# Two attention layers on one core: first key columns loaded first, and another order of copies, tables and products in the last passes

## Chip, core and metric

The kernel runs on one core of a Trainium2 chip. The metric is the time of one execution in microseconds (us) on the device. Before the change three runs gave 904.05, 904.2 and 906.41 us; the median is 904.2 us. All data are float32. Engines are called as in the profile: PE (TensorE's matrix products, PEld its weight loads), DVE (VectorE), ACT (ScalarE), POOL (GpSimd), SP (SyncE, which here only issues transfers). ACT and POOL issue transfers too.

## What is computed

Two cross-attention layers, one after the other, for 8 batches of 256 tokens with 320 channels, 20 heads of 16 channels, and a context of 256 tokens of 512 channels. Cut to what matters:

```python
# layer 0: first 77 context tokens are text, the other 179 image tokens
q = split(x @ Wq.T); k, v = split(text @ Wk.T), split(text @ Wv.T)
k_ip, v_ip = split(ip @ Wk_ip.T), split(ip @ Wv_ip.T)
a = softmax(q @ k.T / 4) @ v + softmax(q @ k_ip.T / 4) @ v_ip
x = x + merge(a) @ Wo.T + bo
# layer 1: first 252 context tokens are text, the last 4 image tokens
probs_t = softmax(q @ k_t.T / 4)
text_out = probs_t @ v_t
qsem = l2norm(probs_t @ text_ehs)                 # 512 channels per head and token
fused = q @ k_ip.T / 4 + 0.5 * (qsem @ l2norm(ip_ehs).T)
ip_out = (softmax(fused) * spatial_mask) @ v_ip
x = x + merge(text_out + ip_out) @ W_out + b_out
```

## The kernel before the change

**Work.** A unit is one batch, one layer and a quad of four heads. There are 40 units per layer (8 batches, 5 quads). The main loop (L1155) runs n from 0 to 45. For n below 40, `both_layers` (L1078) does unit n of layer 0 and, six steps behind (SHIFT), a unit of layer 1. For n = 40 to 45, `layer_1` (L1123) does layer 1 alone: n = 40 the last quad of batch 6, n = 41 to 45 the five quads of batch 7. `l1_end` (L863) finishes the last quad and the output of batch 7. Other work (projections, transposes, outputs) is put between the steps by `fillers` (L976), a table of functions by step and place: in n = 40 transposes, projections and keys, in n = 41 queries and keys, in n = 44 transposes and outputs; n = 42, 43 and 45 have no or hardly any PE work there.

**Order.** The order on PE, DVE, ACT and POOL is the program's own order. An engine runs its instructions one after the other and waits at each for what it needs. SP's order is chosen by the framework. Transfers are issued by SP, ACT and POOL, each in its own queue; eight semaphores for the transfers of SP and ACT are used in turn, so that a transfer can wait for an earlier one to land before it is issued.

**Start.** SP loads xT and encT of batch 0, then x and texts. ACT's queue (L160 to L166) loads wq, wk, wkip, the tails of wk and wkip (64 channels of layer 1's keys, L120), wv and wvip. The tile of wk holds 4 blocks of 128 rows with 320 + 64 columns. PE does q (`project_q`, L270; 12 PE instructions, since each float32 product is two), then 128 channels of keys (`project_k`, L288: a part with wk, a part with wkip), ACT copies them (L445), POOL makes a masked query (L332, tile qz, two buffers), and the scores of a quad follow (`scores`, L335), then the values v (`project_rows`, L302). Later loads are issued by POOL (`load_late`, L957).

**A unit of layer 1.** Its steps, with their lines:

- scores (L342): 16 PE instructions into four PSUM tiles sc, one per head j, with both halves of the tokens;
- `l1_max` (L693): per head one DVE reduction for the negative maximum (L696);
- `l1_exp` (L706): per head and half one exponential on ACT with its sum (L711; here "exp j0" means both halves of head 0);
- `l1_image_scores` (L688): per head a copy of the image scores out of sc (tile aip, L691);
- `l1_transposed` (L719, L380): four transposes per head, which write over sc, and a copy out (et, L387);
- `l1_values` (L722): per head and half a product y (L735 and L738) in one of two PSUM buffers, a DVE step e that multiplies and sums it (L742), and a copy of 20 numbers out of it (num, L746). A buffer is free for the next but one y when e and num of its y are done.

In `layer_1` a pass runs the scores, maxima, exponentials and transposes of its own unit u1, and the values of the unit before, v1. The order is:

```python
for pair in range(2):
    l1_max(u1, pair, False)
    l1_values(v1, pair, (0,), nc.scalar.copy)
    l1_exp(u1, pair)
    l1_values(v1, pair, (1,))
    fillers(n, 2 + pair)
```

then the four aip copies on ACT, place 4, the values of head 2, all four transposes with place 5 between them, the values of head 3, place 6.

**The end.** `l1_end` splits the 20 heads into the first 16 and the last 4. For each part: `l1_den` (L760) and `l1_norm` (L766: a DVE step L771, a square root on ACT L773, and a dummy exponential L776 that brings back ACT's table for Exp), `l1_text` (POOL, L814), `l1_fused` and `l1_fused_exp` (L785 to L794), `l1_probs` (L796), `l1_probs_T` (transposes L828, copy L835). The sums of text and image are made on PE: products of the text part with the identity (L884), then products with the image part (L893); `keep` copies them out (L902), `project` (L905) multiplies with Wo, L950 adds the residual, and SP and ACT store. ACT holds one table of functions at a time; a change between square root and exponential is a load (ACT_TABLE_LOAD).

Of the kernel before, what the change touches and what calls it, by code (L numbers as in the profile page):

```python
# [8 lines left out]
F32 = mybir.dt.float32  # L9
# [4 lines left out]
P = 128  # L14
# [3 lines left out]
NE = E // P  # L18
# [32 lines left out]
def kernel(  # L51
# [40 lines left out]
    def mm_tile(name):  # L92
        return ps_mm.tile([P, 512], F32, tag="mm", name=name)
# [15 lines left out]
    def new_e(name, pool=const, tag=None, again=0):  # L109
        return pool.tile([P, NE, C + again], F32, tag=tag or name, name=name)  # L110
# [5 lines left out]
    def load_e(t, w, eng):  # L116
        n = min(C, t.shape[2])
        eng.dma_start(out=t[:, :, 0:n], in_=w[:, 0:n].rearrange("(k p) c -> p k c", p=P))

    def load_tail(t, w, eng):  # L120

        eng.dma_start(
            out=t[:, :, C:], in_=w[:, C - HP :].rearrange("(k p) c -> p k c", p=P)
        )

    def load_xT(b, eng):
# [22 lines left out]
    wo, wo1 = new_c("wo"), new_c("wo1")  # L149


    wk, wkip = new_e("wk", again=HP), new_e("wkip", again=HP)
    wk1 = const.tile([P, NE, C - HP], F32, tag="wk1", name="wk1")

    wv, wvip, wv1 = new_e("wv"), new_e("wvip"), new_e("wv1", again=NIP)
# [2 lines left out]
    bo_b = const.tile([P, C], F32, tag="bo_b", name="bo_b")  # L158
    bo1_b = const.tile([P, C], F32, tag="bo1_b", name="bo1_b")
    load_c(wq, WqT, nc.scalar)  # L160
    load_e(wk, WkT, nc.scalar)
    load_e(wkip, WkipT, nc.scalar)
    load_tail(wk, Wk1, nc.scalar)
    load_tail(wkip, Wk1, nc.scalar)
    load_e(wv, WvT, nc.scalar)
    load_e(wvip, WvipT, nc.scalar)  # L166

    ident = const.tile([P, P], F32, tag="ident", name="ident")
    make_identity(nc, ident)
# [38 lines left out]

    def columns(w, k, m):

        return w[:, k, m * P : (m + 1) * P]

    twice(wq)
# [476 lines left out]
        ip = 0 if u["t0"][x] else TXT1  # L690
        copy(bat[u["b"]]["aip"][:, :, h, :], sc[:, :, ip : ip + NIP])  # L691

    def l1_max(u, x, image=True):  # L693
        t0 = u["t0"][x]
        for j in range(2):
            nc.vector.tensor_reduce(  # L696
                u["nmx"][x][:, j, :],
                u["sc"][2 * x + j][:, :, t0 : t0 + TXT1],
                AX.X,
                ALU.max,  # L700
                negate=True,
            )
            if image:
                l1_image_scores(u, x, j, nc.vector.tensor_copy)

    def l1_exp(u, x):  # L706
        t0 = u["t0"][x]
        for j in range(2):
            h = QUADS[u["g"]][1][2 * x + j]
            for half in range(NH):  # L710
                nc.scalar.activation(  # L711
                    u["e"][x][:, j, half, t0 : t0 + TXT1],
                    u["sc"][2 * x + j][:, half, t0 : t0 + TXT1],
                    AF.Exp,
                    bias=u["nmx"][x][:, j, half : half + 1],
                    accum_out=bat[u["b"]]["den1"][:, half, h : h + 1],
                )

    def l1_transposed(u, j, copy=None):  # L719
        transposed_probs(u, j, TC1, u["t0"][j // 2], copy)  # L720
# [39 lines left out]
    def l1_den(b, hs=ALL):  # L760
        r = bat[b]
        den = r["den1"][:, :, hs]
        nc.vector.reciprocal(by_head(r, "rden1", b)[:, :, hs], den)
        nc.vector.tensor_tensor(by_head(r, "nrm", b)[:, :, hs], den, den, ALU.mult)

    def l1_norm(b, hs=ALL):  # L766
        r = bat[b]
        n2 = r["n2"][:, :, hs]

        nrm = by_head(r, "nrm", b)[:, :, hs]  # L770
        nc.vector.scalar_tensor_tensor(nrm, nrm, EPS2, n2, ALU.mult, ALU.max)  # L771

        nc.scalar.activation(nrm, nrm, AF.Sqrt, scale=1.0 / SEM_SCALE**2)  # L773

        one = small.tile([P, 1], F32, tag="one", name=f"one_{b}", bufs=1)
        nc.scalar.activation(one, msk[:, 0:1], AF.Exp)  # L776

    def l1_fused(b, hs=ALL, eng=nc.gpsimd):
        r = bat[b]
# [38 lines left out]
                ALU.mult,  # L818
            )

    def l1_probs_T(b, hs=ALL, ps=None):
        r = bat[b]

        rows = hs.stop * NIP
        if ps is None:
            ps = mm_tile(f"pT_{b}")
        for half in range(NH):
            nc.tensor.transpose(  # L828
                ps[:rows, half * P : (half + 1) * P],
                r["fus"][:, half, : hs.stop, :].rearrange("p h k -> p (h k)"),  # L830
                ident,
            )
        if "pT" not in r:
            r["pT"] = small.tile([H * NIP, NH * P], F32, tag="pT", name=f"pT_sb_{b}", bufs=1)
        nc.vector.tensor_copy(r["pT"][:rows], ps[:rows, : NH * P])  # L835

    def l1_attn(b):
        r = bat[b]
# [24 lines left out]
    def l1_end(b, u):  # L863

        r = bat[b]
        first, last = slice(0, 16), slice(16, H)

        def tile(j, name):
            return ps_sc.tile([P, NH * S], F32, tag=f"sc{j}", name=f"end_{name}")

        def values(j, half):
            l1_values(u, j, (half,), nc.scalar.copy)
# [12 lines left out]

        def image(ps, ms, hs):
            rows = hs.stop * NIP  # L890
            vip = r["vip"].rearrange("p h d -> p (h d)")[:rows]
            for i, m in enumerate(ms):
                nc.tensor.matmul(  # L893
                    ps[:, i * S : (i + 1) * S], chunk(vip, m), r["pT"][:rows],
                    start=False, stop=m == ms[-1],
                )

        def keep(ps, ms):
            n = len(ms)
# [13 lines left out]
        o = [tile(2 + half, f"o_{half}") for half in range(NH)]  # L913
        l1_den(b)
        l1_norm(b, first)
        values(0, 0)
        l1_text(b, first)
        values(0, 1)
        l1_fused(b, first)
        values(1, 0)  # L920
        values(1, 1)
        l1_fused_exp(b, first)
        sums = tile(0, "aT")
        text(sums, (0, 1))
        values(2, 0)
        values(2, 1)
        l1_probs(b, first)
        values(3, 0)
        values(3, 1)
        l1_norm(b, last)  # L930
        l1_text(b, last)
        l1_probs_T(b, first, tile(1, "pT"))
        l1_fused(b, last, nc.vector)
        l1_fused_exp(b, last, nc.vector)
        image(sums, (0, 1), first)
        keep(sums, (0, 1))
        sums = mm_tile("end_aT2")
        text(sums, (2,))
        l1_probs(b, last, nc.vector)
        project(0, 0)  # L940
        project(0, 1)
        project(1, 0)
        l1_probs_T(b, last, tile(1, "pT2"))
        project(1, 1)
        image(sums, (2,), last)
        keep(sums, (2,))
        for half, eng in enumerate((nc.sync, nc.scalar)):
            project(half, 2)
# [118 lines left out]
    def part(f, u, *args):  # L1067
        if u is not None:
            f(u, *args)
# [53 lines left out]
    def layer_1(n, u, v1):  # L1123


        fillers(n, 0)
        fillers(n, 1)
        part(l0_attn, u)
        u1 = begin1(n)

        if (n + 1 - SHIFT) % NQ:
            qz[1] = queries(1, n + 1)
        for pair in range(2):
            l1_max(u1, pair, False)
            l1_values(v1, pair, (0,), nc.scalar.copy)
            l1_exp(u1, pair)
            l1_values(v1, pair, (1,))
            fillers(n, 2 + pair)
        for head in range(4):
            l1_image_scores(u1, head // 2, head % 2, nc.scalar.copy)  # L1140
        fillers(n, 4)
        part(l1_values, v1, 2)
        for head in range(4):
            if head == 2:
                fillers(n, 5)
            part(l1_transposed, u1, head, nc.scalar.copy)
        part(l1_values, v1, 3)
        fillers(n, 6)
        return None, u1

    l0_q(0, (0, 1))
# [77 lines left out]
```

## Time and profile before

| What | Value |
|---|---|
| median of three runs | 904.2 us |
| the profiled execution: its time | 902.27 us |
| its span in the profile | 900.6 us |
| PE busy | 867.4 us (96%) |
| DVE, ACT, POOL busy | 606.3 (67%), 550.1 (61%), 221.8 us (25%) |
| from 0 to 16.3 us: PE busy | 8.17 us |
| from 797.0 to 877.4 us: PE busy | 76.17 of 80.40 us |
| from 877.4 to 900.6 us: PE busy | 15.81 of 23.20 us |
| exponential of layer 1 (L711), 128 x 252 | 484 ns |
| maximum of layer 1 (L696), 128 x 504 | 673 ns |
| e (L742) and num on DVE (L746) | 418 and 174 ns |
| a table load on ACT | 1.28 us |

A line of the merged timeline gives start in us, length in us, engine, line, operation, written tile <- read tiles, shapes and count, and in brackets the idle time of the engine before it with what ended it. A line of the stretches gives length, busy time of PE, PEld, DVE, ACT and POOL with counts, the granted clock of PE, the mean share of the DMA engines and GB/s. A line of a DMA queue gives packets, MB and the share of 16 engines that the packets took. The chain of waits is followed back from the last instruction; its shares tell which engine's work set the end.

### The profile page before, as it was taken

What the parts mean: (1) busy time and instruction counts of PE and PEld (TensorE: products, weight loads), DVE (VectorE), ACT (ScalarE), POOL (GpSimd) and SP (SyncE); (2) the same over time, 40 slices, a digit from 0 to 9 for tenths busy, and PEclk for the clock granted to TensorE, in tenths of its full rate; (3) what the DMA queues carried; (4) which work ended last, traced back from release to release, by engine and by line L of the source; (5) the groups of instructions that cost most, each with busy time, mean ns of one, the idle gap of its engine ahead of it and who ended that gap; (6) DMA issues with size and microseconds to landing.
All of it is one profiled execution on the core that took longest, in us unless ns stands there. A gap on an engine that the chain in (4) does not pass through costs nothing.

```text
span 900.6 us, 18697 instructions
## 1 busy us (share of the span) xinstructions
PE 867.4 (96%) x6170; PEld 696.6 (77%) x6170; DVE 606.3 (67%) x2043; ACT 550.1 (61%) x2406; POOL 221.8 (25%) x397
## 2 busy tenths in 40 slices
PE   6999899999999999999999999999999999899996
PEld 4767678788777888788887788878877887678774
DVE  1454477767776777776777677776687767874664
ACT  3775666646654686556766468555775557745663
POOL 5522311213211232132221223212221223212201
PEclk9999999999999999999999999999999999999998
DMA  9500100001000100001001010001000100000000
GB/s 298 143 6 1 56 2 1 1 16 42 15 2 21 33 24 2 20 17 42 15 1 21 16 43 1 1 20 34 24 1 11 25 1 2 1 20 1 1 20 16
DMA packets 21072, 22.96 MB, mean 25 GB/s; under 512 B 5856, under 2 KB 20128, under 8 KB 20976
## 3 DMA queue, kind: packets, MB, share of 16 engines
q1 hardware_dynamic: 15072, 13.27, 5.8%
q10 hardware_dynamic: 4608, 4.38, 1.6%
q0 software_dynamic: 1296, 4.12, 1.5%
q8 instruction: 50, 0.82, 0.4%
q14 instruction: 46, 0.38, 0.1%
HBM read 18.31 MB, written 2.62 MB: 23 GB/s over the span
## 4 chain that ended last, share of the span: by engine, by line
PE 80%; ACT 6%; DVE 2%; issue 1%; POOL 0%; ACTq 0%; DVEq 0%
PE y L735 15%; PE sc L380 15%; PE sc L342 8%; PE v L305 8%; PE y L738 8%; PE k L293 6%; PE q L275 6%; PE p_o L318 5%; PE oT L513 4%; ACT e L495 2%; ACT e L711 2%; PE g L604 2%; PE p_aT_ps L311 1%; PE ipo L842 1%; PE o L533 1%
## 5 line engine op out<-in xcount | busy, mean ns | idle before, releaser
L495 ACT ACTIVATE e<-sc,nmx 128x77 f32<-128x77 f32 (+1 forms) x640 | 227.1, 411 | 57.5 <-DVE nmx L483 57.5
L711 ACT ACTIVATE e<-sc,nmx 128x252 f32<-128x252 f32 x320 | 147.0, 484 | 103.4 <-DVE aip L691 103.4
L735 PE MATMUL y<-gv,et 126*128 126x272 f32 x640 | 202.9, 398 | 5.0 <-ACT num L746 4.4
L742 DVE CUSTOM_DVE_ANT_0 e<-y,e 128x252 f32<-128x252 f32 x320 | 133.4, 418 | 108.2 <-PE y L738 96.4
L380 PE MATMUL sc<-ident,e 128*126 128x128 f32 (+1 forms) x1280 | 182.8, 275 | 11.8 <-ACT e L495 6.5
L483 DVE TENSOR_REDUCE nmx<-sc 128x2 f32<-128x154 f32 x320 | 109.6, 414 | 91.5 <-PE sc L342 91.5
L380 PEld LDWEIGHTS sc<-ident,e 128*126 128x126 f32 (+1 forms) x1280 | 148.1, 140 | 25.1 <-ACT e L495 12.5
L387 DVE COPY et<-sc 128x512 f32<-128x512 f32 (+1 forms) x222 | 149.9, 688 | 26.0 <-PE sc L380 16.8
L495 ACT ACTIVATION_READ_ACCUMULATOR e<-sc,nmx 128x1 f32 x640 | 159.7, 250 | 0.0
L738 PEld LDWEIGHTS y<-gv,et 126*128 126x128 f32 x640 | 121.1, 189 | 26.0
L738 PE MATMUL y<-gv,et 126*128 126x146 f32 x640 | 131.9, 288 | 0.0
L735 PEld LDWEIGHTS y<-gv,et 126*128 126x128 f32 x640 | 105.3, 191 | 22.7 <-ACT num L746 6.8
L548 POOL TENSOR_TENSOR attn<-o_sb 128x64 f32<-128x64 f32 x80 | 24.5, 327 | 396.9 <-DVE o_sb L538 357.0
L696 DVE TENSOR_REDUCE nmx<-sc 128x2 f32<-128x504 f32 x160 | 105.6, 673 | 24.2 <-PE sc L342 24.2
L387 ACT COPY et<-sc 128x512 f32<-128x512 f32 (+1 forms) x98 | 55.9, 587 | 75.4 <-PE sc L380 75.4
L342 PE MATMUL sc<-k,sc_qz 32*128 32x256 f32 x1152 | 83.4, 400 | 1.3 <-POOL sc_qz L332 0.8
L332 POOL TENSOR_SCALAR sc_qz<-q,quad_m 128x256 f32<-128x256 f32 x80 | 73.2, 926 | 10.2 <-ACT q L282 9.9
L342 PEld LDWEIGHTS sc<-k,sc_qz 32*128 32x128 f32 x1152 | 52.9, 184 | 24.7 <-issue 14.4
L711 ACT ACTIVATION_READ_ACCUMULATOR e<-sc,nmx 128x1 f32 x320 | 70.0, 219 | 0.0
L305 PE MATMUL v<-wv,encT 128*126 128x324 f32 (+1 forms) x192 | 58.1, 446 | 0.3 <-DMA wv<-in_WvT_dram 0.3
L318 PE MATMUL p_o<-wo,p_aT 128*128 128x320 f32 x180 | 52.8, 437 | 0.3 <-DVE p_aT L312 0.3
L746 DVE COPY num<-y 128x20 f32<-128x20 f32 x300 | 52.2, 174 | 0.0
(159 smaller groups left out, 1053.8 us busy)
## 6 DMA issues: line engine op xcount, KB each, us to landing
encT<-in_encT_dram SPq DMA_DIRECT2D x7, 512.0 KB
x<-in_x_dram SPq DMA_DIRECT2D x8, 320.0 KB
out_dram<-osb SPq DMA_DIRECT2D x15, 160.0 KB
xT<-in_xT_dram SPq DMA_DIRECT2D x7, 256.0 KB
texts<-in_encT_dram SPq DMA_DIRECT2D x6, 154.0 KB
xT<-in_xT_dram SPq DMA_DIRECT2D x7, 128.0 KB
vip_rows<-vipA SPq DMA_DIRECT2D x32, 25.0 KB
wk<-in_WkT_dram ACTq DMA_DIRECT2D x1, 640.0 KB
```

The costliest lines, as they stand in the source:

```text
L305: nc.tensor.matmul(ps, lhsT(k), w[:, k, :], start=(k == 0), stop=(k == NE - 1))
L318: nc.tensor.matmul(ps[:, :C], aT[:, m, :], w[:, m, :], start=(m == 0), stop=(m == NC - 1))
L342: nc.tensor.matmul(sc[j][:, half, :], qz[rows, half * P : (half + 1) * P], kT(j)[rows, :], start=True, stop=True,)
L380: nc.tensor.transpose(v[:, c, half, :], u["e"][x][:, i, half, t0 + c * tn : t0 + (c + 1) * tn], ident,)
L387: copy(u["et"][x][:tn, i].rearrange("p c n s -> p (c n s)"), ps)
L483: nc.vector.tensor_reduce(u["nmx"][x][:, j, :, a], u["sc"][2 * x + j][:, :, t0:t1], AX.X, ALU.max, negate=True,)
L495: nc.scalar.activation(u["e"][x][:, j, half, t0:t1], u["sc"][2 * x + j][:, half, t0:t1], AF.Exp, bias=u["nmx"][x][:, j, half, a : a + 1], ...
L696: nc.vector.tensor_reduce(u["nmx"][x][:, j, :], u["sc"][2 * x + j][:, :, t0 : t0 + TXT1], AX.X, ALU.max, negate=True,)
L711: nc.scalar.activation(u["e"][x][:, j, half, t0 : t0 + TXT1], u["sc"][2 * x + j][:, half, t0 : t0 + TXT1], AF.Exp, bias=u["nmx"][x][:, j, ...
L735: nc.tensor.matmul(y, et[:, 1 - odd, half, :], gv[0][:, g, full], start=True, stop=False)
L738: nc.tensor.matmul(y[:, into], et[:, odd, half, :], gv[1][:, g, part], start=False, stop=True)
L742: nc.vector.tensor_tensor_reduce(e, y[:, g0 : g0 + TXT1], e, op0=ALU.mult, op1=ALU.add, scale=1.0, scalar=0.0, accum_out=r["n2"][:, half, ...
```

## The change

At the start, wk and wkip become lists of two tiles: the first 128 columns, and the other 192 with the 64 tail columns. ACT issues wq and the two first tiles only; wv, wvip and the second tiles are issued by SP, behind encT and ahead of x and texts. Four products of zeros are put on PE ahead of q, and a dummy exponential on ACT ahead of its first copy. In the passes of layer 1 alone, maximum, exponentials and values go head by head with num of half 0 on DVE and of half 1 on ACT, and the values of head 2 come between the transposes of heads 0, 1 and of heads 2, 3; `l1_den` of the last batch is moved into the last pass. In `l1_end` num of heads 0 and 1 is copied by DVE, the square root's table is loaded by a dummy right after the first exponential, the identity products move behind the first part's transposes, and the last copy of pT is shared by DVE and ACT.

```diff
+    def load_part(t, at, w, c0, c1, eng):
         eng.dma_start(
-            out=t[:, :, C:], in_=w[:, C - HP :].rearrange("(k p) c -> p k c", p=P)
+            out=t[:, :, at : at + c1 - c0], in_=w[:, c0:c1].rearrange("(k p) c -> p k c", p=P)
         )
...
-    wk, wkip = new_e("wk", again=HP), new_e("wkip", again=HP)
+    wk, wkip = [
+        [const.tile([P, NE, n], F32, tag=f"{name}{n}", name=f"{name}{n}") for n in (P, C + HP - P)]
+        for name in ("wk", "wkip")
+    ]
...
     load_c(wq, WqT, nc.scalar)
-    load_e(wk, WkT, nc.scalar)
-    load_e(wkip, WkipT, nc.scalar)
-    load_tail(wk, Wk1, nc.scalar)
-    load_tail(wkip, Wk1, nc.scalar)
-    load_e(wv, WvT, nc.scalar)
-    load_e(wvip, WvipT, nc.scalar)
+    load_part(wk[0], 0, WkT, 0, P, nc.scalar)
+    load_part(wkip[0], 0, WkipT, 0, P, nc.scalar)
+    load_e(wv, WvT, nc.sync)
+    load_e(wvip, WvipT, nc.sync)
+    for w, given in ((wk, WkT), (wkip, WkipT)):
+        load_part(w[1], 0, given, P, C, nc.sync)
+        load_part(w[1], C - P, Wk1, C - HP, C, nc.sync)
+
+    zeros = work.tile([P, S], F32, tag="qz", name="zeros", bufs=2)
+    nc.vector.memset(zeros, 0.0)
+    ps = mm_tile("zeros")
+    for i in range(4):
+        nc.tensor.matmul(ps[:, :S], zeros[:, :P], zeros, start=True, stop=True)
+
+    one = small.tile([P, 1], F32, tag="one", name="one", bufs=1)
+    nc.vector.memset(one, 0.0)
+    nc.scalar.activation(one, one, AF.Exp)
...
     def columns(w, k, m):
+        if isinstance(w, list):
+            w, m = (w[0], 0) if m == 0 else (w[1], m - 1)
         return w[:, k, m * P : (m + 1) * P]
...
+    def table(func):
+        one = small.tile([P, 1], F32, tag="one", name="one", bufs=1)
+        nc.scalar.activation(one, msk[:, 0:1], func)
...
-        nc.vector.tensor_copy(r["pT"][:rows], ps[:rows, : NH * P])
+        if shared:
+            for copy, cols in ((nc.vector.tensor_copy, slice(0, P)), (nc.scalar.copy, slice(P, 2 * P))):
+                copy(r["pT"][:rows, cols], ps[:rows, cols])
+        else:
+            nc.vector.tensor_copy(r["pT"][:rows], ps[:rows, : NH * P])
...
-        l1_den(b)
         l1_norm(b, first)
-        values(0, 0)
         l1_text(b, first)
-        values(0, 1)
+        values(0, nc.vector.tensor_copy)
         l1_fused(b, first)
-        values(1, 0)
-        values(1, 1)
+        values(1, nc.vector.tensor_copy)
         l1_fused_exp(b, first)
-        sums = tile(0, "aT")
-        text(sums, (0, 1))
-        values(2, 0)
-        values(2, 1)
+        table(AF.Sqrt)
+        values(2, nc.scalar.copy)
         l1_probs(b, first)
-        values(3, 0)
-        values(3, 1)
+        values(3, nc.scalar.copy)
         l1_norm(b, last)
         l1_text(b, last)
         l1_probs_T(b, first, tile(1, "pT"))
         l1_fused(b, last, nc.vector)
         l1_fused_exp(b, last, nc.vector)
+        sums = tile(0, "aT")
+        text(sums, (0, 1))
         image(sums, (0, 1), first)
...
-        l1_probs_T(b, last, tile(1, "pT2"))
+        l1_probs_T(b, last, tile(1, "pT2"), True)
...
         for pair in range(2):
-            l1_max(u1, pair, False)
-            l1_values(v1, pair, (0,), nc.scalar.copy)
-            l1_exp(u1, pair)
-            l1_values(v1, pair, (1,))
+            for j, copy in ((0, nc.vector.tensor_copy), (1, nc.scalar.copy)):
+                l1_max(u1, pair, False, (j,))
+                l1_exp(u1, pair, (j,))
+                l1_values(v1, pair, (j,), copy)
             fillers(n, 2 + pair)
         for head in range(4):
             l1_image_scores(u1, head // 2, head % 2, nc.scalar.copy)
         fillers(n, 4)
-        part(l1_values, v1, 2)
-        for head in range(4):
-            if head == 2:
-                fillers(n, 5)
-            part(l1_transposed, u1, head, nc.scalar.copy)
-        part(l1_values, v1, 3)
-        fillers(n, 6)
+        for pair in range(2):
+            for head in (2 * pair, 2 * pair + 1):
+                l1_transposed(u1, head, nc.scalar.copy)
+            if n == N0 + SHIFT - 1 and pair:
+                l1_den(B - 1)
+            part(l1_values, v1, 2 + pair)
+            fillers(n, 5 + pair)
```

More of the change, by code (lines that the diff above doesn't have):

```diff
@@ L118, in load_e @@
         eng.dma_start(out=t[:, :, 0:n], in_=w[:, 0:n].rearrange("(k p) c -> p k c", p=P))
-    def load_tail(t, w, eng):
+    def load_part(t, at, w, c0, c1, eng):
         eng.dma_start(
-            out=t[:, :, C:], in_=w[:, C - HP :].rearrange("(k p) c -> p k c", p=P)
+            out=t[:, :, at : at + c1 - c0], in_=w[:, c0:c1].rearrange("(k p) c -> p k c", p=P)
         )
@@ L691, in l1_image_scores, with l1_max @@
         copy(bat[u["b"]]["aip"][:, :, h, :], sc[:, :, ip : ip + NIP])
-    def l1_max(u, x, image=True):
+    def l1_max(u, x, image=True, heads=range(2)):
         t0 = u["t0"][x]
-        for j in range(2):
+        for j in heads:
             nc.vector.tensor_reduce(
@@ L704, in l1_max, with l1_exp @@
                 l1_image_scores(u, x, j, nc.vector.tensor_copy)
-    def l1_exp(u, x):
+    def l1_exp(u, x, heads=range(2)):
         t0 = u["t0"][x]
-        for j in range(2):
+        for j in heads:
             h = QUADS[u["g"]][1][2 * x + j]
@@ L773, in l1_norm @@
         nc.scalar.activation(nrm, nrm, AF.Sqrt, scale=1.0 / SEM_SCALE**2)
-        one = small.tile([P, 1], F32, tag="one", name=f"one_{b}", bufs=1)
-        nc.scalar.activation(one, msk[:, 0:1], AF.Exp)
+        table(AF.Exp)
     def l1_fused(b, hs=ALL, eng=nc.gpsimd):
@@ L819, in l1_text, with l1_probs_T @@
             )
-    def l1_probs_T(b, hs=ALL, ps=None):
+    def l1_probs_T(b, hs=ALL, ps=None, shared=False):
         r = bat[b]
@@ L872, in tile, with values @@
             return ps_sc.tile([P, NH * S], F32, tag=f"sc{j}", name=f"end_{name}")
-        def values(j, half):
-            l1_values(u, j, (half,), nc.scalar.copy)
+        def values(j, copy):
+            for half in range(NH):
+                l1_values(u, j, (half,), copy)
         def chunk(t, m):
```

## The prediction

> **What bounds the kernel now.** I read the page's chain first: it says which engine set the end.
>
> ```profile
> PE 80%; ACT 6%; DVE 2%; issue 1%; POOL 0%; ACTq 0%; DVEq 0%
> ```
>
> TensorE carries the end, so an edit counts only where PE waits. The busy time by stretch shows where that is: PE is busy 767.24 of 780.70 us from 16.3 to 797 us, which the diff leaves alone, but 8.17 of 16.30 at the start, 76.17 of 80.40 in the passes of layer 1 alone (n = 40 to 45), 15.81 of 23.20 at the end. Those three are what is edited.
>
> The start, in PE's timeline (start, length, idle before and its releaser):
>
> ```profile
> 5.15 4.46 PE L275 MATMUL q<-xT,wq 128*128 128x256 f32 x12 [5.15 <-DMA wq<-in_WqT_dram]
> 10.42 1.09 PE L293 MATMUL k<-encT,wk 128*128 128x77 f32 x8 [0.81 <-DMA wk<-in_WkT_dram]
> 12.86 1.48 PE L293 MATMUL k<-encT,wkip 128*128 128x179 f32 x8 [1.35 <-DMA wkip<-in_WkipT_dram]
> 14.89 1.15 PE L342 MATMUL sc<-k,sc_qz 32*128 32x256 f32 x16 [0.55 <-ACT k L445]
> 16.30 2.39 PE L305 MATMUL v<-wv,encT 128*128 128x320 f32 x8 [0.27 <-DMA wv<-in_WvT_dram]
> ```
>
> The landing of wkip sets the first scores. The last pass (n = 45), from the merged timeline:
>
> ```profile
> 868.05 1.27 DVE L696 TENSOR_REDUCE nmx<-sc 128x2 f32<-128x504 f32 x2 [0.43 <-PE sc L342]
> ...
> 869.70 0.18 ACT L746 COPY num<-y 128x20 f32<-128x20 f32 x1 [3.42 <-DVE n L742]
> 869.77 0.48 ACT L711 ACTIVATE e<-sc,nmx 128x252 f32<-128x252 f32 x1
> ...
> 869.92 0.72 PE L735 MATMUL y<-gv,et 126*128 126x272 f32 x2 [0.28 <-ACT num L746]
> ...
> 873.73 0.39 ACT L691 COPY aip<-sc 128x8 f32<-128x8 f32 x4
> ...
> 873.97 1.97 PE L380 MATMUL sc<-ident,e 128*126 128x128 f32 x16 [0.20 <-ACT aip L691]
> ```
>
> The transposes (L380) wait for the first image copy (aip), which stands behind all eight exponentials on ACT. While PE waits it does the products y of heads 0, 1 and 2. The end:
>
> ```profile
> 880.65 0.20 ACT L776 ACTIVATE one<-msk 128x1 f32<-128x1 f32 x1
> 880.76 0.23 ACT L746 COPY num<-y 128x20 f32<-128x20 f32 x2
> ...
> 880.97 0.72 PE L735 MATMUL y<-gv,et 126*128 126x272 f32 x2 [1.86 <-ACT num L746]
> ```
>
> PE stands still because the copies that free its two y buffers sit behind a table load. What follows, by stretches (length, busy us of each engine, granted clock, DMA):
>
> ```profile
> 882.00:883.00 1.00, 1.00 (x6) 0.95 (x5) 0.45 (x3) 0.18 (x1) 0.00 (x0) 0.62 0.00 0
> 883.00:884.00 1.00, 1.00 (x6) 1.00 (x6) 0.59 (x3) 0.18 (x1) 0.33 (x1) 0.50 0.00 0
> ```
>
> After 1.86 us without work PE ran for 3.4 us at half clock.
>
> **Part 1, the loads.** ScalarE's queue loses wk, wkip, wv, wvip and two tails, and keeps 128 columns of wk and of wkip; wv, wvip and the rest go to SP ahead of x and texts. How two queues share the DMA engines, from 9.5 to 11.0 us (q10 is ScalarE's, q1 SP's; packets, MB, share):
>
> ```profile
> q10 hardware_dynamic: 315, 0.40, 83.4%
> q1 hardware_dynamic: 314, 0.10, 28.0%
> ```
>
> They take turns packet by packet: 315 packets of 1280 B against 314 of 308 B. A packet costs its engine 0.834 x 24 / 315 = 63.5 ns and 0.280 x 24 / 314 = 21.4 ns. The 1024 B packets of 6.00 to 7.25 us cost 48.6 ns (189 at 45.9% of 20 us); 512 B, between, are estimated at 29. wk and wkip are 1024 packets before and after, 1280 B before and 512 B after. Before, they began at 6.0: 202 went beside 189 of encT until 7.25, 286 beside 214 of x until 9.0, 536 one to one with the 308 B texts: 536 x 84.9 / 16 = 2.84, so 11.84; the product began 1.0 later. After, at the same ratios: 0.94, then (286 x 29 + 214 x 63.5) / 16 = 1.37, then 536 one to one with wv's 1280 B: 536 x 92.5 / 16 = 3.10. Sum 11.4, product at 12.4: 0.45 earlier. What the short rows save, SP's long rows take back. wv no longer lands last (0.27 before L305). I take **-0.7**. Bounds: if the queues shared by bytes, 2 x 0.91 MB would be through at 7.9 us by the GB/s row, and two products of 0.9 and 1.4 would give scores at 11.7, **-3.2**; if nothing lands earlier and the longer idle brings half clock, k and scores gain 1.2, **+1.2**.
>
> Covered: four zero products (eight instructions at 0.43, twice the warm 0.216) end before 5.15 and let q take 2.8 (the row of 2.79 at 143.22) for 4.46, but PE then waits for wk; the early table load (1.28 at 10.71) ended before k did. The remaining columns of wk and wkip stand in SP's queue beside POOL's loads (wk1 at 14.48 first); the DMA ran full until 22.4 and they are needed at 27.7, so nothing, unless over 5 us late. x and texts come later still, and x is used by POOL's adds after 34.65. SP's queue gains waits for reused semaphores: wvip's for xT (landed by 5.15), with all the rest behind it; the others' for wq and encT, which land before their turn. The zeros lie in a masked query's buffer, free long before POOL's second one (13.6).
>
> The Trainium skill ("DMA: Bandwidth & Descriptors", "Issuing engines are not separate DMA queues") says that issuing on several engines saves only issue time. That speaks against this part, and by it the sum would be 0.0 here; the packet counts say that a queue's row size matters, and give -0.7.
>
> **Part 2, the passes.** Now each head's maximum, exponentials and product follow each other, half 0's num copy is on DVE and half 1's on ACT; and heads 0 and 1 are transposed ahead of head 2's y. Times from the start of the scores (866.89). Before: exp 2.88, third y 3.03, fourth y 3.84, aip 6.84, transposes 7.08, last y ends 10.46. After: DVE's first maximum runs 1.16 to 1.83; exp j0 at 1.95 (0.12 later, as from 39.33 + 0.34 + 0.41 = 40.08, where two maxima end in n = 2, to the exponential at 40.20). DVE: e at 2.09, num 2.43, second maximum 2.52 to 3.19; exp j1 at 3.31. Four exps took 1.82 (chain), eight instructions with their sums read, so two take 0.88 to the next start: ACT's num of half 1 starts at 4.19, and **what is queued behind it is the fourth y**, which needs that buffer: 4.42 instead of 3.84, and with 0.1 of restart PE is **0.67** late. DVE's third maximum 3.50, fourth 4.56 to 5.23; exp j2 4.29, exp j3 5.35 to 6.23; num; aip 6.31; transposes 6.55, 0.53 earlier. But the two y of head 2 (0.7 each, 1.42 for both halves) now come after that wait: 1.42 - 0.53 = **0.9** later in a pass with nothing else for PE. In n = 42 ACT starts at 3.03 after its table loads, aip is only 0.11 earlier: **1.3**. n = 40, 41, 44 have PE work (projections, keys) in that gap and lose the 0.67. n = 40 to 44: 3 x 0.67 + 1.3 + 0.9 = **+4.2** (n = 45 is counted below). Bounds: 0, if PE never waits longer; 6 x 1.42 = 8.5, if aip gains nothing.
>
> **Part 3, the end**, same origin. Last y of the pass 11.32 (was 10.46). The norm's DVE step (L771) 11.79 to 12.0 (the two steps ahead of it, L763 and L764, 0.5, are moved out of this chain), sqrt 12.03, exp table until 13.56. The first num copies are DVE's, so y runs on: four end at 14.57. Max 15.04, POOL 15.8, exp 15.85, sqrt table 16.15 to 17.43. Head 2's y run to 16.1; head 3's wait for ACT's num behind that load: 17.76 (1.61 after it begins, as 879.36 to 880.97), idle 1.66 where it was 1.86. They end 19.45; norm step 19.96; sqrt 20.15 without a load; last exp 1.63 later as before, 21.78, was 25.04. PE: transposes 19.85, eight identity products (0.163 each, of 0.71 for 4) 21.2, image 22.25, four identity products 22.9, three projections 1.45: second transposes 24.3, was 26.6. The shared copy (0.29 for 0.42) saves 0.13. **-2.4**, n = 45's loss included. Bounds -4 (1.6 more if the last chain follows exp without PE) to 0 (half clock stays, 1.7, and 0.7 of slips).
>
> **Half clock.** A window of 3.4 us at half clock costs 1.7 where PE is the bound. In n = 42, 43, 45 PE now idles 0.9 (before the fourth y) and 1.16 (before the transposes), 2.06 within 3.0 us; 1.86 brought it on above. I take 1.1 such windows over the three passes: **+1.9**; bounds 0 and 5.1.
>
> The Trainium skill ("TensorE: Matmul & The Clock Gate", "HAM oscillation") warns of gaps above about 3.4 us. By that these gaps cost 0 and the sum is +1.1; the row at 882, after 1.86, says otherwise.
>
> **Sum:** -0.7 + 4.2 - 2.4 + 1.9 = **+3.0**. The profiled execution is 902.27 (span 900.6 and 1.67 around it): 905.3. It lies 1.9 below the median of 904.2, so the forecast for the median is **907.2**.
>
> **Rivals.** (a) *PE keeps full clock in the passes*: +1.1, 905.3. For it: at 11.5 to 12.9 PE idled 1.35 and kept its clock. (b) *Not slower, by the start*: the queues' share follows bytes, wkip lands 3.2 earlier instead of 0.7: 3.0 - 2.5 = +0.5, 904.7, and with (a) -1.4, 902.8. It decides from the start's worth: at -1.0 (wkip's product at 12.1) the sum is down to 2.7; below zero it comes only with (a), from a product before 11.3 (start -1.8). Against it: 315 to 314. (c) *Faster*: the pass loses nothing, since aip moves a whole 1.42 ahead: +3.0 - 4.2 - 0.9 - 1.9 = -4.0, 900.2; DVE's order speaks against it. (d) *The loads do not come earlier at all* and PE is cold for them: +3.0 + 1.9 = 909.1.
>
> **Chances.** Forecast (907 to 908.5) with (d) and more half clock windows, up to 911: 0.52. (a) and the nearer half of (b): 0.33. (c), and (b) with (a) and a better end: 0.15. About 0.3% (2.7 us) is what a measurement can tell from no change: slower 0.52, same 0.33, faster 0.15. Range 901.5 to 911.0.
>
> **What would show it.** Right: wkip's product at 12 to 12.6; in n = 45 the transposes 6.4 to 6.7 after the scores and 1.0 us or more of PE idle before them; 0.6 before the fourth y; one table load fewer at the end, y of head 3 released by ACT's num. Wrong: PE idle before the transposes under 0.5, k at 9 and wkip at 10, or granted clock 1.00 through the passes (then (a)).

## The result, and the profile after

The changed kernel takes 907.56 us (median of 20 runs, 904.24 to 910.75), the kernel before beside it 903.69 us (20 runs, 901.25 to 906.9). The ratio is 1.0038 (95% interval 1.0026 to 1.0049): 3.4 us more (2.3 to 4.4). The profiled execution of the changed kernel is its longest run: 910.75 us, a span of 909.0 and a mean granted clock of 0.990. Before, the profile had 902.27, 900.6 and 0.997.

The first line of the page's chain of waits has the same shares as before (PE 80%, ACT 6%), so PE still sets the end and the three edited stretches can again be read one by one.

*The start*, PE's timeline after (start, length, idle before and its releaser):

```profile
1.24 3.78 PE L177 MATMUL zeros<-zeros 128*128 128x256 f32 x8 [1.24 <-DVE one L180]
5.24 3.21 PE L292 MATMUL q<-xT,wq 128*128 128x256 f32 x12 [0.22 <-DMA wq<-in_WqT_dram]
9.94 1.09 PE L310 MATMUL k<-encT,wk 128*128 128x77 f32 x8 [1.48 <-DMA wk<-in_WkT_dram]
12.54 2.52 PE L310 MATMUL k<-encT,wkip 128*128 128x179 f32 x8 [1.52 <-DMA wkip<-in_WkipT_dram]
15.62 2.09 PE L359 MATMUL sc<-k,sc_qz 32*128 32x256 f32 x16 [0.55 <-ACT k L462]
17.63 3.40 PE L322 MATMUL v<-wv,encT 128*128 128x320 f32 x8
```

The two key products begin 0.48 and 0.32 us earlier (before: 10.42 and 12.86), and the values wait for no load. But the wkip product lasts 2.52 us where it lasted 1.48, and the scores 2.09 for 1.15: half clock. In the stretches (length, busy us of PE, PEld, DVE, ACT and POOL with counts, granted clock, DMA share, GB/s):

```profile
9.38:12.79 3.41, 1.33 (x9) 1.22 (x10) 0.00 (x0) 0.00 (x0) 3.41 (x5) 1.00 1.09 344
12.79:16.20 3.41, 2.86 (x13) 2.38 (x16) 0.00 (x0) 0.37 (x1) 3.19 (x6) 0.51 1.15 300
16.20:19.62 3.42, 3.42 (x20) 2.13 (x13) 1.93 (x6) 1.07 (x7) 0.51 (x1) 0.50 1.03 359
```

*The last pass* (n = 45; its scores begin at 876.62), merged timeline. The transposes come 6.50 us after the scores where they came 7.08 after; PE stands still 0.72 ahead of the fourth y and 0.98 ahead of the transposes; then y takes 1.11 us, twice its usual time:

```profile
880.93 0.17 ACT L763 COPY num<-y 128x20 f32<-128x20 f32 x1
...
881.16 0.73 PE L752 MATMUL y<-gv,et 126*128 126x272 f32 x2 [0.72 <-ACT num L763]
...
882.87 0.39 ACT L708 COPY aip<-sc 128x8 f32<-128x8 f32 x4
883.12 1.92 PE L397 MATMUL sc<-ident,e 128*126 128x128 f32 x8 [0.98 <-ACT aip L708]
...
884.82 1.11 PE L752 MATMUL y<-gv,et 126*128 126x272 f32 x2
```

The stretches around it, 3.41 us each, tell why. In the first, PE is busy 1.71 of 3.42 us; in the next its clock is 0.50:

```profile
879.77:883.19 3.42, 1.71 (x9) 1.13 (x8) 2.53 (x10) 3.17 (x18) 0.06 (x1) 1.00 0.01 2
883.19:886.60 3.41, 3.41 (x13) 3.14 (x14) 0.03 (x1) 1.25 (x4) 0.00 (x0) 0.50 0.00 0
```

*The end*, merged timeline:

```profile
894.49 1.28 ACT L786 ACT_TABLE_LOAD   x1
...
895.89 0.24 ACT L763 COPY num<-y 128x20 f32<-128x20 f32 x2
...
896.10 0.73 PE L752 MATMUL y<-gv,et 126*128 126x272 f32 x2 [1.56 <-ACT num L763]
...
900.12 0.21 ACT L814 ACTIVATE fus<-fus 128x32 f32<-128x32 f32 x1
```

PE's long wait is still there (1.56 for 1.86), behind the load that was put ahead of the square root; the last exponential comes 10.5 us after the end's first y (889.59), where it came 14.5 after it (877.46 and 891.93).

From the two traces, the difference of 8.4 us in span is +2.3 at the start (first transposes at 23.02 for 20.68), +9.95 in the passes (from the scores of n = 40 to the end's first y: 85.88 for 75.93), -3.7 at the end (19.41 for 23.14), and -0.2 between. Half clock is in all of them: after, two windows at the start, one each in n = 42, 43 and 45; before, one at the end (the last 2 us of each left out).

### The profile page after: what moved, and what is told of

Its sections match the earlier page's. It is cut to its first block, busy times and chain, and to the rows that moved or that the text cites. A ratio compares the mean times of both kernels' runs of the same rounds, so it can differ in the third digit from the quotient of the medians.

```text
span 909.0 us, 18730 instructions
## 1 busy us (share of the span) xinstructions
PE 876.2 (96%) x6178; PEld 703.0 (77%) x6178; DVE 606.4 (67%) x2049; ACT 550.9 (61%) x2405; POOL 222.0 (24%) x397
## 3 DMA queue, kind: packets, MB, share of 16 engines
q10 hardware_dynamic: 2496, 2.02, 0.7%
## 4 chain that ended last, share of the span: by engine, by line
PE 80%; ACT 6%; DVE 2%; issue 1%; POOL 0%; ACTq 0%; DVEq 0%
PE y L752 15%; PE sc L397 15%; PE sc L359 8%; PE v L322 8%; PE y L755 8%; PE k L310 6%; PE q L292 6%; PE p_o L335 5%; PE oT L530 4%; ACT e L512 2%; ACT e L728 2%; PE g L621 2%; PE p_aT_ps L328 1%; PE ipo L866 1%; PE o L550 1%
## 5 line engine op out<-in xcount | busy, mean ns | idle before, releaser
L397 PE MATMUL sc<-ident,e 128*126 128x128 f32 (+1 forms) x1280 | 185.5, 277 | 14.2 <-ACT e L512 6.5
```

The source lines that it names most:

```text
L397: nc.tensor.transpose(v[:, c, half, :], u["e"][x][:, i, half, t0 + c * tn : t0 + (c + 1) * tn], ident,)
```

## The experiments

Every run has a mean granted clock, so span x (1 - clock) gives half the time that it spent at half clock, which is what that can have cost. Of the kernel before, 89 runs were taken beside the experiments; they show what a loss of clock costs:

| Mean clock of the run | Runs of before | Their mean time, us |
|---|---|---|
| 0.999 to 1.000 | 10 | 901.1 |
| 0.998 | 17 | 902.6 |
| 0.996 | 18 | 904.3 |
| 0.994 | 11 | 904.4 |
| 0.992 | 29 | 905.8 |

(The other 4, at 0.997, took 902.5.) Below, a ratio is to the runs of before beside it, and us are 904.3 x (ratio - 1). It is not the ratio of the two medians; where these say something else by 1 us or more, both are given.

**e1_before_again.** No edit.

> The kernel before, unchanged, for the clock of each of its runs. Its profile had one window of half clock at the end (882 to 885.7 us) and the beginning of one in its last 1.3 us: 1.7 + 0.7 = 2.4 us lost, a mean clock of 0.997. Theory: its own runs of 901 to 907 us differ by such windows (each 3.4 us at half clock, 1.7 us lost), so that time less span x (1 - clock) is the same in all of them, near 899.9 us. Rival: they differ by something else, and the sum of time and clock loss spreads as the times do.

Measured: 904.38 us (901.22 to 906.04), ratio 1.0003 (0.9987 to 1.0019). The runs at clock 0.999 take 901.3 us, those at 0.992 take 905.9. So they do differ by half clock; but time less clock loss is not constant (900.4 and 898.6), since PE waits in part of such a window anyway. Its profile has two windows at the start and two in the end. At the start PE was busy 1.81 us of the window ahead:

```profile
9.35:12.76 3.41, 1.81 (x12) 1.27 (x10) 0.00 (x0) 1.88 (x2) 0.00 (x0) 1.00 1.15 314
12.76:16.18 3.42, 2.75 (x8) 2.29 (x8) 0.00 (x0) 0.37 (x1) 3.33 (x4) 0.50 1.14 318
```

In the first profile of before the window from 11.84 to 15.25 had 1.84 busy, and full clock after it: nearly the same share, and the other outcome. So the median run of before has more half clock in it than the profile that I predicted from.

**e2_start_only.** Of the change only the start: load_part, the two tiles each of wk and wkip, the queues, the products of zeros, the dummy exponential, and columns.

> Only the start of the change (loads, products of zeros, early table load). Prediction: -0.7 us. In the profile after, wkip's product began 0.32 us earlier and the values waited for no load, but half clock from 12.8 to 19.6 us made it +2.3 by the first transposes. Theory: that window is rare (the other 19 runs after have a clock that leaves no room for two more windows), so -0.6 us in the median, clock as in the kernel before. Rival: the products of zeros start the clock's windows earlier, half clock falls on the keys in most runs, and it is +1.0 to +2.5 us, with the clock lower by 0.002 to 0.004.

Measured: 903.34 us, ratio 0.9999 (0.9982 to 1.0016). Its one run at clock 1.000 took 900.05, 1.1 less than before at such a clock; but 10 of its 12 runs are at 0.996 or less. In its profile the values begin at 15.87 (16.30 before), without half clock at the start. By the times alone a gain of 0.7 can't be told from nothing (the medians, 903.34 and 904.39 beside it, differ by 1.0). The profiles say more of the loads: wkip's product begins at 12.51 on the mean of the eight with this start and nothing put into its gaps (12.15 to 12.76), and at 12.93 in the four with the old one (12.86 to 13.06). So the loads come 0.42 earlier (0.45 forecast), and where half clock falls on the start, as in the profile after, it takes back more than that; neither theory alone holds.

**e3_passes_only.** Of the change only the loop over pairs in layer_1 (and the argument heads).

> Only the new order in the passes of layer 1 alone (n = 40 to 45). Prediction: +4.2 and 0.9 for n = 45, so +5.1 at full clock, and +1.9 from 1.1 windows of half clock: +7.0 us. From the profile after: +4.8 at full clock and three windows, +5.1, so up to +9.9 us in some runs. Rival: the passes cost under +2 at full clock and the loss sits in the start.

Measured: 912.43 us (6 runs), ratio 1.0105 (1.0081 to 1.0129): +9.5 us (7.3 to 11.7). The passes are the loss, not the start. It is more than the 7.0 forecast, which lies just below the interval (by the medians, 912.43 and 904.39, it is +8.0); its profiled run, the slowest (916.11, clock 0.987), has two windows at the start, three in the passes and two at the end.

**e4_end_only.** Of the change only l1_end, table and the shared copy; l1_den moved into the last pass:

```diff
+        if n == N0 + SHIFT - 1:
+            l1_den(B - 1)
         part(l1_values, v1, 3)
```

> Only the end of the change (numerators, tables and products in l1_end; the reciprocals of l1_den in the last pass). Prediction: the second part's last exponential 3.3 us earlier, no window of half clock at 882 us: -3.3 us. In the profile after the end took 19.41 us from the first y to the last instruction, against 23.14: -3.7, of which 1.7 is the window. Rival: it is bound by the chain after the last exponential, and gains under 1.5 us.

Measured: 899.6 us, ratio 0.9963 (0.9948 to 0.9978): -3.3 us (by the medians, 899.6 and 904.39, -4.8). Median clock 0.999, where before has 0.996: at about equal clock (its two runs at 1.000, 899.0, against 901.1) it is -2.1; the rest goes with windows of half clock that 7 of its 10 runs don't have.

**e5_without_passes.** The changed kernel with the old order in layer_1 (and the two lines above).

> The changed kernel with the passes of before (start and end of the change kept). Theory: the parts add: end only measured -4.8 us in the median (-2.6 between the runs with hardly any half clock, 898.6 against 901.2), start only -1.1 between such runs and nothing certain in the median; so 898 to 900 us, 4 to 6 below before. Rival: the end gains only because of the passes ahead of it, or the start costs in company: 901 or more.

Measured: 900.79 us, ratio 0.9959 (0.9943 to 0.9974): -3.7 us. So the passes turn a change that gains 3.7 us into one that loses 3.4. The start adds hardly anything to the end (0.9963 in e4): 7 of its 8 runs have a clock of 0.994 to 0.996 and take 899.9 to 901.3; the eighth, at 0.999, takes 897.84.

**e6_gaps_filled.**

```diff
+        def fill(products):
+            if n in (42, 43, 45):
+                ps = mm_tile(f"fill_{n}_{products}")
+                for i in range(products):
+                    nc.tensor.matmul(ps[:, :P], ident, ident, start=True, stop=True)
...
+                if pair and j:
+                    fill(2)
                 l1_values(v1, pair, (j,), copy)
...
         fillers(n, 4)
+        fill(3)
```

> The changed kernel with products of the identity on PE in its two idle gaps of n = 42, 43 and 45: two ahead of the fourth y (idle 0.72), three ahead of the transposes (idle 0.98). Results are as before, PE only has something to do. Theory: the gaps bring on windows of half clock, three in the profile after (842, 856, 883 us); filled, they go, the clock of the runs rises from 0.993 to 0.997 and more, and the median falls by 3 to 4 us to about 904; the products cost at most 0.2 a gap. Rival: the windows come from elsewhere or cost nothing: 907.5 or more, clock 0.993.

Measured: 905.64 us, ratio 1.0016 (1.0001 to 1.0030): +1.4 us, 2.0 less than the changed kernel (0.3 to 3.7). PE's timeline in n = 45 (scores at 872.99): the products take the idle time, the transposes come as late as ever (6.49 after the scores), and the y after them run at full speed:

```profile
877.52 0.72 PE L752 MATMUL y<-gv,et 126*128 126x272 f32 x2 [0.28 <-ACT num L763]
...
878.34 0.83 PE L1158 MATMUL fill<-ident 128*128 128x128 f32 x6
879.48 1.09 PE L397 MATMUL sc<-ident,e 128*126 128x128 f32 x8 [0.31 <-ACT aip L708]
880.41 0.62 PE L752 MATMUL y<-gv,et 126*128 126x272 f32 x2
```

No window of half clock is left in its passes. Two at the start are: 11 of its 12 runs have a clock of 0.996 or 0.994, so the clock stays below the 0.997 expected and the median above the 904. The fall itself, 2.0 for the 3 to 4 expected, suggests that the changed kernel's runs have on average fewer windows in the passes than its profile with three. This run gives the bare cost of the order; the time from one pass's scores to the next (for n = 45 to the end's first y), us:

| n | before | after (profile) | after, gaps filled | filled - before | forecast |
|---|---|---|---|---|---|
| 40 | 19.57 | 20.25 | 20.25 | 0.68 | 0.67 |
| 41 | 10.92 | 11.72 | 11.72 | 0.80 | 0.67 |
| 42 | 10.39 | 13.17 | 11.72 | 1.33 | 1.3 |
| 43 | 11.69 | 14.20 | 12.51 | 0.82 | 0.9 |
| 44 | 12.79 | 13.57 | 13.57 | 0.78 | 0.67 |
| 45 | 10.57 | 12.97 | 11.28 | 0.71 | 0.86 |

Sum 5.12, forecast 5.07. Half clock adds 1.45, 1.69 and 1.69 in the profile.

**e7_values_first.**

```diff
+        part(l1_values, v1, 2)
         for pair in range(2):
             for head in (2 * pair, 2 * pair + 1):
                 l1_transposed(u1, head, nc.scalar.copy)
...
-            part(l1_values, v1, 2 + pair)
+            if pair:
+                part(l1_values, v1, 3)
```

> The changed kernel with head 2's two y ahead of all the transposes, as in the kernel before; all else as changed. Theory: PE then has them to do while it waits for the exponentials. The second y of head 2 waits for ACT's num behind the last exponential, so the transposes start 0.7 us later (7.2 after the scores, not 6.5), but the pass ends 0.8 earlier: -2.4 for n = 42, 43 and 45, and one or two windows of half clock fewer: 902 to 905 us. Rival: what the y gain the later transposes give back: 907 or more.

Measured: 903.58 us, ratio 0.9994 (0.9979 to 1.0008), 4.0 less than the changed kernel. PE's timeline in n = 43 (scores at 844.41): the second y of head 2 waits 0.20, the transposes wait for nothing, 7.22 after the scores.

```profile
850.82 0.72 PE L752 MATMUL y<-gv,et 126*128 126x272 f32 x2 [0.20 <-ACT num L763]
...
851.63 1.04 PE L397 MATMUL sc<-ident,e 128*126 128x128 f32 x8
```

Against the filled kernel n = 42 and 43 are 0.72 shorter each, as expected; n = 45 only 0.15, because there that y waits 0.81, by the profile for a DVE num. Why is open.

**e8_num_dve.**

```diff
-            for j, copy in ((0, nc.vector.tensor_copy), (1, nc.scalar.copy)):
+            for j, copy in ((0, nc.vector.tensor_copy), (1, nc.vector.tensor_copy)):
```

> The changed kernel with num of both halves on DVE in the passes, so that the fourth y doesn't wait for ACT behind exp j1. Theory: the fourth y starts 0.5 to 0.6 earlier; that is a gain in n = 40, 41 and 44, which have PE work behind it, but in n = 42, 43 and 45 the transposes wait for the last exponential, which comes 0.25 later because DVE has the copies ahead of its maxima: -1.7 and +0.8, about -1.0 us. Rival: the wait of the fourth y is a loss in every pass: -3.5 to -4.

Measured: 905.51 us, ratio 1.0020 (1.0006 to 1.0034), 1.6 less than the changed kernel (0 to 3.3). The wait ahead of the fourth y is gone; n = 40, 41 and 44 are 0.43, 0.44 and 0.21 shorter; in n = 45 (scores at 873.19) the whole idle time now stands ahead of the transposes, which come 0.34 later:

```profile
880.03 1.09 PE L397 MATMUL sc<-ident,e 128*126 128x128 f32 x8 [2.02 <-ACT aip L708]
```

So in the bare passes (n = 42, 43 and 45) PE loses by the wait for all eight exponentials; the wait of the fourth y is part of it, not added to it.

**e9_early_transposes.** The kernel of e5 with this order of a pass, shown without the lines that it replaces (e10: max, values and exponentials by pairs as before, the same aip copies and transposes):

```diff
+        for pair in range(2):
+            for j in range(2):
+                l1_max(u1, pair, False, (j,))
+                l1_exp(u1, pair, (j,))
+                l1_values(v1, pair, (j,))
+            for j in range(2):
+                l1_image_scores(u1, pair, j, nc.scalar.copy)
+            fillers(n, 2 + pair)
+        fillers(n, 4)
+        for pair in range(2):
+            for head in (2 * pair, 2 * pair + 1):
+                l1_transposed(u1, head, nc.scalar.copy)
...
+            part(l1_values, v1, 2 + pair)
+            fillers(n, 5 + pair)
```

> Start and end of the change, and another order of a pass: maxima, exponentials and values go head by head as in the change, with num of both halves on DVE; each pair's aip copies come on ACT right behind its exponentials, so that heads 0 and 1 can be transposed before head 2's y, and heads 2 and 3 after it, without waiting for all eight exponentials. Theory: what cost the change its pass is the y put behind the last exponential; here the first transposes start about 4.4 us after the scores and a bare pass ends at about 9.3 (10.57 before, 13.0 to 13.2 after in half clock): 3 x 1.2 less than without the passes of the change, 897 us, and no half clock in the passes. Rival: DVE (four maxima, eight e, eight num, 8.1 us of work in 9.3) becomes the bound and a pass ends no earlier than before: 900 or more.

Measured: 898.78 us, ratio 0.9939 (0.9923 to 0.9955). The passes take 74.39 us against 75.82 in e5; n = 45 takes 9.41 (expected 9.3), but n = 40, 41, 43 and 44 gain nothing like that. In n = 43 PE waits 0.64 for POOL's fus instead.

**e10_pairs_early.**

```diff
         for pair in range(2):
             l1_max(u1, pair, False)
             l1_values(v1, pair, (0,), nc.scalar.copy)
             l1_exp(u1, pair)
+            for j in range(2):
+                l1_image_scores(u1, pair, j, nc.scalar.copy)
             l1_values(v1, pair, (1,))
             fillers(n, 2 + pair)
```

> Start and end of the change, the order of before by pairs of heads, with each pair's aip copies right behind its four exponentials and the transposes of heads 0 and 1 ahead of head 2's y. Theory: first transposes at about 5.0 us, a bare pass ends at 9.75, 0.8 earlier than before: 898.5 us. Rival: ACT's num of head 1 waits between the exponentials for DVE behind two maxima, the last exponential comes at 7.5, and nothing is gained: 900.5 or more.

Measured: 898.34 us, ratio 0.9934 (0.9916 to 0.9951). PE's timeline in n = 45 (scores at 868.71): the first transposes 4.91 after the scores, the last y ends at 9.7, both as expected.

```profile
873.62 1.09 PE L397 MATMUL sc<-ident,e 128*126 128x128 f32 x8 [0.19 <-ACT aip L708]
874.54 0.62 PE L752 MATMUL y<-gv,et 126*128 126x272 f32 x2
...
875.96 1.04 PE L397 MATMUL sc<-ident,e 128*126 128x128 f32 x8
```

Only two heads' exponentials stand ahead of the first transposes, and each y has a transpose or another y to wait beside.

**e11_start_filled.** The kernel of e5 with

```diff
+    cold = [0, 1]
...
+        fill = mm_tile("fill") if cold else None
         ps = mm_tile(f"{name}_{m}")
         for w, t0, t1, rhs in parts:
+            if cold:
+                cold.pop()
+                for i in range(5):
+                    nc.tensor.matmul(fill[:, :P], ident, ident, start=True, stop=True)
```

> Start and end of the change, passes of before (as in the kernel without the passes, 900.8 us), and five products of the identity on PE ahead of each of the two first key products, where PE idles 1.48 and 1.52 us. Theory: the start of the change gained nothing in the median because its idle gaps bring two windows of half clock at 12 to 19 us in most runs (a clock of 0.996 or less in 7 of 8 runs, 2.2 to 3.4 us more than the run without). Filled, they go: clock 0.999, 898 us. Rival: the windows come from the wait for loads in some other way: still 0.994 to 0.996 and 900.5 us.

Measured: 897.9 us (897.67 to 898.12, 5 runs), ratio 0.9932 (0.9918 to 0.9946), clock 1.000 in every run. PE's timeline:

```profile
8.23 1.28 PE L315 MATMUL fill<-ident 128*128 128x128 f32 x10
10.46 1.09 PE L317 MATMUL k<-encT,wk 128*128 128x77 f32 x8 [0.96 <-DMA wk<-in_WkT_dram]
11.38 1.32 PE L315 MATMUL fill<-ident 128*128 128x128 f32 x10
13.08 1.48 PE L317 MATMUL k<-encT,wkip 128*128 128x179 f32 x8 [0.37 <-DMA wkip<-in_WkipT_dram]
```

In this profile the loads came late (13.08 for wkip's product, 0.57 after the mean of the eight), yet the ratio is 0.0027 below that of e5, 2.4 us (0.5 to 4.3; by the medians 2.9): the gain over e5 comes from the filled gaps, not from earlier loads. The spread of the times fell with it, from 3.4 us in e5 to 0.5.

**e12_together.** e10 and e11, and in l1_end

```diff
-        values(2, nc.scalar.copy)
+        values(2, nc.vector.tensor_copy)
```

> What helped, together: start of the change with its gaps filled (897.9 us with the passes of before), the passes by pairs with early aip copies and transposes (73.92 us from the scores of n = 40 to the first y of the end, 1.9 less than 75.83 with the passes of before), the end of the change, and in it num of head 2 on DVE, so that head 3's y don't wait for ACT behind the load of the square root's table (idle 1.57 in every run with that end). Theory: the parts add, since PE is the bound in each stretch: 897.9 - 1.9 - 1.3 = 894.7 us, clock 1.00. Rival: the gap at the end only moves (the transposes then wait for POOL's fus, 0.6 us after the last y): 896.0 us.

Measured: 895.68 us (895.33 to 895.98), ratio 0.9911 (0.9896 to 0.9926): 8.0 us less than before, the best version. The end takes 18.84 us for 19.46: 0.6 of the 1.3, as the rival said, since the transposes now wait for POOL:

```profile
882.62 0.41 PE L855 MATMUL end_pT<-ident,fus 128*64 128x128 f32 x2 [0.76 <-POOL fus L830]
```

## Why the prediction was right, step by step

The forecast was 907.2 us, the result 907.56; +3.0 forecast against the profile of before, +3.4 (2.3 to 4.4) measured. By parts:

| Step | Forecast | Measured |
|---|---|---|
| start, loads | -0.7 | -0.1 (-1.6 to 1.4) by the ratio, -1.0 by the medians (e2); values begin 0.11 to 0.79 earlier than in the profile of before where the start has full clock (e2, e9, e11, e12) |
| passes, with n = 45 | +5.1 | +5.12 in the filled trace; +5.2 by times (e6 against e5, 0.0016 + 0.0041) |
| end | -3.3 | -3.3 (-4.7 to -2.0) by the ratio, -4.8 by the medians (e4) |
| half clock in the passes | +1.9 | +2.0 (0.3 to 3.7) (after against e6) |

**The loads.** Packet by packet was right. From 7.25 to 9.0 us, with q1 carrying wv and q10 wk and wkip (packets, MB, share):

```profile
q1 hardware_dynamic: 327, 0.42, 73.7%
q10 hardware_dynamic: 336, 0.17, 36.8%
```

A 512 B packet took 0.368 x 28 / 336 = 30.7 ns (29 estimated), wkip's product began at 12.54 (12.4 forecast). Rival (b), sharing by bytes, would have needed 10. The Trainium skill ("DMA: Bandwidth & Descriptors", "Issuing engines are not separate DMA queues") allows only issue time as a gain. Here wkip's product came 0.42 us earlier on the mean (12.51 for 12.93), but the loads ahead of it were made shorter too, so no run tests that sentence alone.

**What failed here** is the bound of the start: I let half clock cost at most +1.2 there and gave it no place in the sum, without a reason; only rival (a) names a row, the 1.35 us of idle time in the profile of before through which PE kept its clock. That row was a near thing: the run had 1.84 of 3.41 us busy in the window that mattered, and in two other runs of the same start a window with 1.81 (e1) and 1.83 (e3) was followed by half clock. The change has 1.33 in its profile, and 1.09 to 1.49 in five of the other seven with its start. With the new start 28 of 32 runs (e5, e6, e9, e10; 10 of 12 in e2, 8 of 12 in e7) have a clock of 0.996 or less, with the old start and the new end (e4) 3 of 10. How much of the -0.7 this takes the times don't tell (e2's interval holds both 0 and -0.7; e5 against e4 is -0.4 by the ratios, +1.2 by the medians); filling the gaps gained 2.4 (e11). Rival (d) had it in part: the loads do come earlier, but PE is cold for them. That it did not spoil the total is chance: the median of before has such windows too (a clock of 0.996, not the 0.997 of its profile), which I carried over as a plain offset of 1.9 us.

**The passes.** The table by n shows each term. The fourth y started 4.54 after the scores (4.42 forecast), the transposes 6.50 (6.55). In n = 45 at full clock the end's first y came 11.28 after the scores, where I had the last y end at 11.32. Rival (c) needed aip to move 1.42 ahead; it moved 0.58. The two y of head 2 behind that wait are most of the loss in n = 43: e7, which puts them ahead, takes back 0.72 of 0.82 there. In n = 42 it takes back 0.72 of 1.33 and in n = 45 0.15 of 0.71; what the rest is there no run shows.

**The end.** The last exponential was forecast 21.78 after the last scores: 900.12 - 876.62 = 23.50, less 1.69 of half clock in n = 45, is 21.81. That the time agrees to the tenth is chance: ratio and medians of e4 are 1.5 apart. Head 3's y stood 1.56 (1.66). The sign "one table load fewer" was wrong as I wrote it: there are four loads at the end before and after. One was moved ahead of the last chain, which was what the sum used.

**Half clock.** In the profile after, windows with 1.61, 1.71 and 1.70 us busy of 3.41 (from 838.85, 852.50 and 879.81) were each followed by half clock, in all three bare passes; I had 1.1 of three. e6 against the changed kernel gives +2.0 by the ratios, which is 1.2 windows at 1.7, but its interval also allows two. How often each pass is hit can't be told from the runs, whose clocks add the start's windows to the passes'. It also matters how the idle time falls on the windows' edges: in n = 45 of e8 the wait of 2.02 us lies across two windows, which are busy 2.05 and 2.59 us (from 875.79 and 879.21), and no half clock followed. Rival (a), full clock in the passes, forecast 905.3; e6, which makes it so, measured 905.64. The Trainium skill ("TensorE: Matmul & The Clock Gate", "HAM oscillation") puts the danger at gaps above about 3.4 us; here gaps of 0.72 and 0.98 us in one such window were enough. Its section "Part 1: The HAM clock gate" has a free-running window of 3413 ns, and that length agrees with the 3.41 us in these records.

**The signs** of the forecast: wkip's product within 12 to 12.6, yes; transposes 6.4 to 6.7 after the scores, yes; 1.0 us or more idle before them, just missed with 0.98; 0.6 before the fourth y, 0.72; y of head 3 released by ACT's num, yes.

## What to carry to other kernels

Where PE is the bound, list what it can do during each wait before an order is changed: an instruction that is moved behind the wait can cost its full time, even if the wait itself gets shorter. Count PE's busy share in windows of the clock's length as well as its idle time, at the start of a kernel too; a few products of no use in a gap can be worth more than the transfer that is brought forward (e11, 2.4 us). Read the granted clock of many runs before one profile is taken for the kernel.

## What the runs showed of the hardware

The windows are 3.41 us long in the traces, and a run's clock mostly fell to half for one or more of them when PE was busy for about half of the one before or less. In the 14 profiles, the windows of the last output left out, 17 windows with 1.09 to 1.71 us busy (32 to 50%) were followed by half clock, and so were two with 1.81 and 1.83 (the old start in e1 and e3); 19 with 1.84 to 1.90 (54 to 56%) were followed by full clock. Four windows don't fit: after one with 1.69 (e8, n = 43) the clock stayed at 1.00, and after three with 2.21 to 2.28 (65 to 67%), all in the old `l1_end` (e1, e2, e3), it fell to 0.50. In e8 and e1:

```profile
851.90:855.32 3.42, 1.69 (x14) 1.44 (x13) 1.74 (x8) 2.82 (x14) 1.47 (x4) 1.00 0.00 0
...
889.99:893.40 3.41, 2.28 (x12) 1.33 (x10) 1.84 (x9) 2.82 (x5) 1.21 (x4) 1.00 0.00 0
```

So PE's busy share is a good sign of half clock, not the whole rule, and what else counts is open.

Nearly all the spread of the kernel before (901 to 906 us) goes with the mean clock: 10 runs at 0.999 and more took 901.1 us, 29 at 0.992 took 905.8. With the gaps of the start filled and those of passes and end shortened (e12), five runs lie within 0.65 us.
